# A triangle-and-gate pair kernel: the first seven tiles take their transposed input from the host, like all later ones, with other factors, order and queues

## The chip, the core and the metric

The kernel runs on one core of a Trainium2 chip. A core has a matrix engine (TensorE, PE in the profile; its weight loads are the row PEld), three engines for elementwise work (VectorE = DVE, ScalarE = ACT, GpSimd = POOL) and a queue engine (SyncE = SP) that only starts transfers. Each engine works through its own instruction list strictly in order; they wait for each other through semaphores. Transfers between the chip's memory and the on-chip buffers are started from the lists of SP, ACT or POOL. The metric is the device time of one execution in microseconds (us); less is better.

## The reference, cut to what matters

The input `x` is a 384 x 384 array of vectors with 128 channels, all float32. Two layers follow each other. The change touches only the first part of layer 0, written here with its names:

```python
z_n = _layernorm(z, norm_g, norm_b)                 # over the 128 channels
a = _linear(z_n, Wa, ba) * sigmoid(_linear(z_n, Wga, bga))
b = _linear(z_n, Wb, bb) * sigmoid(_linear(z_n, Wgb, bgb))
x = einsum('bijd,bjkd->bikd', a, b)                 # 128 products of 384 x 384 matrices
x = _layernorm(x, normo_g, normo_b)
out = z + _linear(x, Wo, bo) * sigmoid(_linear(z_n, Wgo, bgo))
```

Layer 1 then makes two projections of `out`, left (with the sum of two weight matrices, `W_left + W_eq`) and gate, multiplies them with the row sum of a third, projects the product, adds `out` and normalises.

## The kernel before, in words

The kernel has three stages. Stage 1 computes `a`, `b` and the gate of the output for all pixels and writes them to memory as A, B and G, together with Z = x + an output bias. Stage 2 (from L631) makes the 128 matrix products of A and B. Stage 3 (from L756) does the rest row by row. Only stage 1 is changed, and within it mostly its first tiles.

Stage 1 runs over 72 tiles of 128 rows x 16 columns x 128 channels (1 MB), each in four steps of four columns (512 vectors), so 288 calls of `step(s)` (L284); `n` is the tile and `t` the step in it. The program order of each engine is the order in which the Python code issues (the schedule is manual), so every position in `step` is a position in the engines' lists.

A projection needs the normalised input with the channels on the partitions. This comes about in two ways. In tiles 0 to 2 (`n < OLD`, L104), VectorE takes mean and variance (`statistics`, L154, with `bn_aggr`), POOL makes factor and offset (`norm_factors`, L161), ScalarE normalises column by column (`normalise`, L219), TensorE transposes four columns (`turn`, L238) and ScalarE copies the result out of PSUM (`turned_out`, L247). From tile 3 on, the transposed input `xT` is read from memory, where the host has put it (`fetch_turned`, L149). POOL computes one factor for each pixel from the raw statistics (`turned_factors`, L174, seven small instructions); ScalarE spreads the factors over the partitions with 16 copies of 32 x 16 values (`repeat`, L186); VectorE turns these into a full tile of factors with a 32 x 32 transpose and multiplies (`normalise_turned`, L196). Of the four columns of a step, POOL multiplies two (L216) and VectorE two. That the mean is subtracted is then the weights' work: they are multiplied with a centring matrix (`of_the_turned`, L381, called after steps 4, 5 and 6).

A step (L284 to L370) issues, in this order: on SP the next fetches where a tile begins; the statistics of columns some 36 ahead (VectorE) and the factors (POOL); the projections `ga` and `a` (TensorE, L308); the sigmoid of `ga` (ScalarE, L316); the sigmoid of the output gate of the step before (L257) and, after a tile, the store of G (started by POOL, L260); `at` (VectorE, L333) and, after a tile, the store of A (POOL, L337); `gb` and its sigmoid; in steps with `t == 1` the 16 copies; in the first tiles transpose and normalisation; `b` and `bt` (VectorE, L349); the output gate's projection (`gate_project`, L262: eight small products, L271, and `gs`, L273); the normalisation of step s+2; and the residual (`residual`, L229), which is one POOL addition over the whole tile (L235) followed by the start of the store of Z (L236). PSUM has six banks for the projections (`ppp`) and two for the transposes (`ppt`).

The buffer of an `x` tile is free once its statistics and its residual are done; there are three, so `fetch(n + 3)` waits for the residual of tile n. In the first 12 steps the residuals, factors and fetches have places of their own (`FIRST_RESIDUALS`, `FIRST_FACTORS`, `FIRST_FETCHES`, L278 to L283); later a tile's factors are issued at `t == 0` and its residual at `t == 1`.

Before step 0 (L411 to L467) the first quarter of tile 0 is loaded and normalised, the weights are scaled by `norm_g`, biases are corrected, and TensorE is kept busy with idle transposes (`keep_busy`, L443). `last_weights` (L393) prepares weights of layers 0 and 1 after steps 24, 25 and 26; among them are two additions of `W_left + W_eq` and of their biases on VectorE:

```python
nc.vector.tensor_tensor(w_left, w_left, w_eq, ALU.add)   # L399
nc.vector.tensor_tensor(b_left, b_left, b_eq, ALU.add)   # L400
```

Of the kernel before, what the change touches and what calls it, by code (L numbers as in the profile page):

```python
# [20 lines left out]
def kernel(ctx: ExitStack, tc: tile.TileContext, ins, out: bass.AP):  # L21
# [82 lines left out]
    OLD, SQ = 3, 32  # L104
# [6 lines left out]
    with tc.tile_pool(name="wprep", bufs=6) as wp, tc.tile_pool(name="p1s", bufs=3) as ps, tc.tile_pool(  # L111
        name="p1g", bufs=2
    ) as pgt, tc.tile_pool(name="p1z", bufs=4) as pz, tc.tile_pool(name="p1a", bufs=2) as pa_, tc.tile_pool(
        name="p1x", bufs=3
    ) as px, tc.tile_pool(name="p1b", bufs=1, side="right") as pb_, tc.tile_pool(name="p1t", bufs=2, space=PSUM) as ppt, tc.tile_pool(
        name="p1p", bufs=6, space=PSUM
    ) as ppp:
        tiles, turned, bts, gated, b_out_of = {}, {}, {}, {}, []

# [8 lines left out]
        def fetch_parts(n, parts):  # L128
# [10 lines left out]
            if n < OLD:  # L139
                tiles[n]["mv"] = ps.tile([P, CX, 2], FP, tag="mv", name=f"mv_{n}")  # L140
            else:
                tiles[n]["again"] = ps.tile([P, CX, P // SQ], FP, tag="again", name=f"again_{n}", bufs=2)
# [6 lines left out]
        def fetch_turned(n):  # L149
            if OLD <= n < NT:  # L150
                tiles[n]["zT"] = pz.tile([P, CX, P], FP, tag="zT", name=f"xT_{n}")
                nc.sync.dma_start(out=tiles[n]["zT"], in_=xT[n])

        def statistics(first, last):  # L154
            for k in range(first, min(last, NT * CX)):
                n, c = divmod(k, CX)
                nc.vector.bn_stats(tiles[n]["st"][:, c, :], tiles[n]["x"][:, c, :])
                if n < OLD:
                    nc.vector.bn_aggr(tiles[n]["mv"][:, c, :], tiles[n]["st"][:, c, :])

        def norm_factors(n, c0=0, c1=CX, beside=nc.gpsimd):  # L161
            if n >= NT:
                return
            if n >= OLD:
                return turned_factors(n, c0, c1)
            mv, rstd, off = (tiles[n][k][:, c0:c1] for k in ("mv", "rstd", "off"))
            beside.tensor_scalar(rstd, mv[:, :, 1], EPS, None, ALU.add)
            beside.tensor_scalar(off, mv[:, :, 0], -1.0, None, ALU.mult)
            nc.gpsimd.tensor_tensor(rstd, rstd, mhalf[:, 0 : c1 - c0], ALU.pow)
            nc.gpsimd.tensor_tensor(off, off, rstd, ALU.mult)  # L170
            if c0 == 0:
                tiles[n]["zT"] = pz.tile([P, CX, C], FP, tag="zT", name=f"zn_{n}")

        def turned_factors(n, c0, c1):  # L174

            st, v, d = (tiles[n][k][:, c0:c1] for k in ("st", "rstd", "off"))
            g = nc.gpsimd
# [6 lines left out]
            g.tensor_tensor(v, v, mhalf[:, 0 : c1 - c0], ALU.pow)  # L184

        def repeat(n):  # L186

            if n >= NT:
                return
            for b in range(P // SQ):  # L190
                for to in range(P // SQ):
                    nc.scalar.copy(
                        tiles[n]["again"][to * SQ : (to + 1) * SQ, :, b], tiles[n]["rstd"][b * SQ : (b + 1) * SQ, :]
                    )

        def normalise_turned(s):  # L196
# [6 lines left out]
            H = CT // 2 if s < S2 else 0  # L203
            for engine, k0, k1 in ((nc.gpsimd, 0, H), (nc.vector, H, CT)):
                if k0 == k1:
                    continue
                if k0 < H:
                    every = ps.tile([P, H, P], FP, tag="every", name=f"every_{s}")
# [10 lines left out]
        def normalise(n, t, cs=range(CT)):  # L219
            if n >= OLD:  # L220
                return
            g = tiles[n]
            for c in (t * CT + k for k in cs):
                nc.scalar.activation(
                    g["zT"][:, c, :], g["x"][:, c, :], AF.Identity,
                    bias=g["off"][:, c : c + 1], scale=g["rstd"][:, c : c + 1],
                )

# [8 lines left out]

        def turn(s, between=None):  # L238
            n, t = divmod(s, TS)
            ptr = ppt.tile([P, CT, P], FP, tag="ptr", name=f"ptr_{s}")  # L240
            for c in range(CT):
                nc.tensor.transpose(ptr[:, c, :], tiles[n]["zT"][:, t * CT + c, :], ident)
                if between:
                    between()
            turned[s] = ptr

        def turned_out(s):  # L247
            n, t = divmod(s, TS)
            zT = tiles[n]["zT"][:, t * CT : (t + 1) * CT, :]
            nc.scalar.copy(zT, turned[s])  # L250
            turned[s] = zT
# [11 lines left out]
        def gate_project(s):  # L263
# [8 lines left out]
            gs = ps.tile([P, CT, C], FP, tag="gs", name=f"gs_{s}")  # L272
# [4 lines left out]
        CATCH_UP = 3 * TS  # L277
        FIRST_FACTORS = {  # L278
            0: ((1, 0, 4),), 1: ((1, 4, 8),), 2: ((1, 8, 12),), 3: ((1, 12, 16),),
            4: ((2, 0, 4),), 5: ((2, 4, 12),), 6: ((2, 12, 16),), 7: ((3, 0, 8),), 9: ((3, 8, 16),),  # L280
        }
        FIRST_RESIDUALS, FIRST_FETCHES = {2: 0, 5: 1, 9: 2, 10: 3}, {2: 3, 5: 4, 9: 5}

        def columns_ahead(s):  # L284
            return CX + CT * s + 2 * min(max(s - TS, 0), 2 * TS)

        def step(s):
            n, t = divmod(s, TS)
            r0, c0 = place(n)
            if t == 0:  # L290
                if n >= OLD:
                    fetch(n + 3)
                fetch_turned(n + 2)
                if s >= CATCH_UP:
                    norm_factors(n + 1)
# [8 lines left out]
            ahead = (n + 1, t - 1) if t else (n, TS - 1)  # L304
# [14 lines left out]
            def statistics_ahead():  # L319
                statistics(columns_ahead(s), columns_ahead(s + 1))  # L320
                for factors in FIRST_FACTORS.get(s, ()):
                    norm_factors(*factors)

            if s:
# [6 lines left out]
            if 0 < s <= S2:  # L331
                gate(s - 1)
            nc.vector.scalar_tensor_tensor(  # L333
                at[:, t * CT : (t + 1) * CT, :], pa, bcol["a"], sga, ALU.add, ALU.mult
            )
            if t == TS - 1:
                nc.gpsimd.dma_start(out=A[:, c0 : c0 + CX, r0 : r0 + P], in_=at)  # L337
            pgb = proj("gb")
            sgb = sigmoid("b", pgb, by_row=True)
            if t == 1 and n + 1 >= OLD:  # L340
                repeat(n + 1)
            if s + 1 < OLD * TS:
                turn(s + 1)
                turned_out(s + 1)
            if s == 0:
                normalise(0, 2)
            normalise(*ahead)
# [6 lines left out]
            if s == 0:  # L354

                statistics_ahead()
            if s + 2 >= OLD * TS:
                normalise_turned(s + 2)
            if s < CATCH_UP:
                if s in FIRST_RESIDUALS:  # L360
                    residual(FIRST_RESIDUALS[s])
                if s in FIRST_FETCHES:
                    fetch(FIRST_FETCHES[s])
            elif t == 1:
# [12 lines left out]
        def scale_weight(k):  # L377
            raw[k], wT[k] = wT[k], ctile([P, P], "wT_" + k)
            nc.scalar.activation(wT[k], raw[k], AF.Copy, scale=ng)

        def of_the_turned():  # L381

            nc.vector.tensor_scalar(center, ident, -1.0 / C, None, ALU.add)
            yield
            for some in (("ga", "a"), ("gb", "b", "go")):
                centred = ppp.tile([P, CT, P], FP, tag="pk", name="centred_" + some[0])
                for n, k in enumerate(some):
                    nc.tensor.matmul(centred[:, n, :], lhsT=center, rhs=wT[k], start=True, stop=True)
                for n, k in enumerate(some):
                    nc.scalar.copy(wT[k], centred[:, n, :])  # L390
                yield

        def last_weights():  # L393
# [5 lines left out]
            nc.vector.tensor_tensor(w_left, w_left, w_eq, ALU.add)  # L399
            nc.vector.tensor_tensor(b_left, b_left, b_eq, ALU.add)  # L400
# [653 lines left out]
```

## Time and profile before

| | |
|---|---|
| median of three runs | 3198.97 us (3198.86 to 3198.99) |
| the profiled execution | 3198.7 us, of which 3196.9 us span |
| mean granted TensorE clock | 0.998 |
| busy shares of the span | PE 99%, DVE 85%, POOL 75%, ACT 63% |
| stage 1 | until about 1278 us, when the first product of stage 2 starts |
| one step of stage 1 in the steady part | 4.33 us |

Times of instructions are microseconds from the start of the span, followed by the duration. "x2" says that the profile shows two records for one instruction of the program. In brackets stands the time that the engine was idle just before, and which engine or transfer ended that idle time. Instructions overlap by a few hundredths to tenths of a microsecond, so the distance from one start to the next is what an instruction takes of its engine's time. PE is busy nearly throughout the span; the few places where it is not lie in the first 160 us, around 1235 and 1250 us, and at the very end.

### The profile page before, as it was taken

Reading aid. Unit: us, or ns where it says so; the run is one execution under the profiler, and the core shown is the slowest. Engines: PE = TensorE matmul, PEld = TensorE weight load, DVE = VectorE, ACT = ScalarE, POOL = GpSimd, SP = SyncE. Lnnn points to the kernel's source line nnn. Section 1 sums busy time; section 2 is a strip of 40 time slices with the busy share of each in tenths; the row PEclk is TensorE's granted clock in tenths of the full one; section 3 lists DMA queues with packets and bytes.
Section 4 is the critical chain, followed back from the end, with each engine's and each line's share of the span. In section 5 each row is a group of like instructions: output and inputs, shape, how many; then the busy total and the mean of one; then the engine's idle time right before and its main releaser. Section 6 shows DMA issues by size and latency. Waiting matters only on the chain.

```text
span 3196.9 us, 51440 instructions
## 1 busy us (share of the span) xinstructions
PE 3166.8 (99%) x14543; PEld 2087.0 (65%) x14543; DVE 2705.2 (85%) x8297; ACT 2008.9 (63%) x5225; POOL 2402.4 (75%) x2097
## 2 busy tenths in 40 slices
PE   9999999999999999999999999999999999999998
PEld 5555555555555555555555555788888888888886
DVE  6999999999999998455555555999999999999999
ACT  7566666666666665222222222588888888888888
POOL 6788888888888885455555555599999998888888
PEclk9999999999999999999999999999999999999999
DMA  6989999999999999999999999777777777777774
GB/s 217 368 341 363 370 369 367 361 362 353 372 370 364 369 363 335 350 314 311 313 311 313 310 309 290 248 267 264 259 268 262 259 270 257 260 270 258 263 269 156
DMA packets 426554, 982.75 MB, mean 307 GB/s; under 512 B 39696, under 2 KB 334224, under 8 KB 381088
## 3 DMA queue, kind: packets, MB, share of 16 engines
q1 hardware_dynamic: 385344, 752.64, 67.9%
q0 software_dynamic: 40352, 226.57, 18.0%
q8 instruction: 118, 1.93, 0.2%
q14 instruction: 164, 1.34, 0.1%
q10 hardware_dynamic: 576, 0.26, 0.0%
HBM read 526.39 MB, written 452.98 MB: 306 GB/s over the span
## 4 chain that ended last, share of the span: by engine, by line
PE 96%; POOL 1%; ACT 1%; DVE 1%; issue 1%; DMA 0%; ACTq 0%; POOLq 0%; DVEq 0%
PE pm L689 23%; PE py L529 8%; PE pf L797 8%; PE pleft L823 8%; PE pg L825 8%; PE pgo L271 8%; PE pga L308 7%; PE pgb L308 7%; PE pa L308 7%; PE pb L308 7%; PE ptr L552 4%; PE pg L836 0%; POOL rstd L184 0%; POOL acc L235 0%; ACT res L815 0%
## 5 line engine op out<-in xcount | busy, mean ns | idle before, releaser
L689 PE MATMUL pm<-ab 128*128 128x384 f32 x2304 | 743.9, 486 | 0.0
L709 POOL TENSOR_TENSOR acc<-acc,xd 128x384 f32<-128x384 f32 x381 | 379.8, 997 | 362.3 <-DVE xd L702 362.0
L689 PEld LDWEIGHTS pm<-ab 128*128 128x128 f32 x2304 | 437.5, 190 | 303.8
L707 ACT ACTIVATE sq<-xd 128x384 f32<-128x384 f32 x381 | 188.4, 495 | 541.3 <-DVE xd L702 541.3
L702 DVE TENSOR_TENSOR xd<-pm,acc 128x384 f32<-128x384 f32 x381 | 212.1, 557 | 342.8 <-POOL acc L709 321.7
L815 ACT ACTIVATE res<-res,off,rs 128x128 f32<-128x128 f32 x1134 | 475.0, 486 | 0.9
L316 ACT ACTIVATE sga<-pga,c_L_conv_bga 128x512 f32<-128x512 f32 x288 | 197.8, 687 | 345.6 <-PE pga L308 343.9
L535 DVE SCALAR_TENSOR_TENSOR py<-py,acc,gr 128x128 f32<-128x128 f32 x1152 | 384.1, 333 | 0.9
L271 PEld LDWEIGHTS pgo<-wT_go,xT 128*128 128x128 f32 x2208 | 287.6, 192 | 124.8 <-issue 78.4
L848 POOL TENSOR_TENSOR res<-res,r_L_conv_ln_bias 128x1536 f32<-128x1536 f32 (+1 forms) x96 | 326.6, 3402 | 7.5
L847 POOL TENSOR_TENSOR res<-res,r_L_conv_ln_scale 128x1536 f32<-128x1536 f32 (+1 forms) x96 | 326.8, 3405 | 0.5 <-ACT res L815 0.5
L235 POOL TENSOR_TENSOR acc<-xt,r_L_conv_b_out 128x2048 f32<-128x2048 f32 x72 | 326.7, 4538 | 0.0
L529 PE MATMUL py<-w_o,xr 128*128 128x128 f32 x2304 | 320.0, 275 | 0.0
L830 ACT ACTIVATE sg<-pg,c_L_conv_b_gate 128x384 f32<-128x384 f32 x384 | 223.0, 581 | 152.1 <-PE pg L825 103.0
L797 PE MATMUL pf<-w_o,h 128*128 128x128 f32 x2280 | 316.8, 275 | 0.0
L823 PE MATMUL pleft<-pairT,m_L_conv_W_left 128*128 128x384 f32 x768 | 311.6, 487 | 0.4 <-ACT pairT L553 0.4
L825 PE MATMUL pg<-pairT,m_L_conv_W_gate 128*128 128x384 f32 x768 | 310.6, 486 | 0.0
L540 DVE BATCH_NORM_STATS2 st<-res 128x6 f32<-128x128 f32 x1128 | 306.7, 272 | 0.0
L216 POOL TENSOR_TENSOR xT<-every,xT 128x256 f32<-128x256 f32 x260 | 190.2, 732 | 141.5 <-DVE every L212 136.0
L529 PEld LDWEIGHTS py<-w_o,xr 128*128 128x128 f32 x2304 | 288.4, 192 | 0.8
L271 PE MATMUL pgo<-wT_go,xT 128*128 128x128 f32 x2208 | 288.7, 275 | 0.0
L308 PE MATMUL pga<-xT,wT_ga 128*128 128x512 f32 x552 | 283.8, 596 | 4.9 <-POOL xT L216 3.2
(189 smaller groups left out, 6578.0 us busy)
## 6 DMA issues: line engine op xcount, KB each, us to landing
Z<-acc POOLq DMA_DIRECT2D x72, 1024.0 KB, 10.7
A<-at POOLq DMA_DIRECT2D x72, 1024.0 KB, 13.5
gr<-G SPq DMA_DIRECT2D x96, 768.0 KB, 5.8
zr<-Z SPq DMA_DIRECT2D x96, 768.0 KB, 7.2
xr<-X SPq DMA_DIRECT2D x96, 768.0 KB, 8.2
X<-xd SPq DMA_DIRECT2D x381, 192.0 KB, 5.8
xt<-in_x_dram SPq DMA_DIRECT2D x71, 1024.0 KB, 7.6
out_dram<-res SPq DMA_DIRECT2D x93, 768.0 KB, 4.1
```

What stands on the lines that cost most here:

```text
L235: nc.gpsimd.tensor_tensor(zb, tiles[n]["x"], over(b_out, CX), ALU.add)
L271: nc.tensor.matmul(pgo[:, c, :], lhsT=zT[:, c, :], rhs=wT["go"], start=True, stop=True)
L308: nc.tensor.matmul(pk, lhsT=wT[k], rhs=zT, start=True, stop=True)
L529: nc.tensor.matmul(py[:, q, :], lhsT=g["x"][:, i, q * P : (q + 1) * P], rhs=w_o0, start=True, stop=True)
L535: nc.vector.scalar_tensor_tensor(py[:, q, :], py[:, q, :], rs0[:, q, u : u + 1], g["g"][:, i, q, :], ALU.mult, ALU.mult)
L689: nc.tensor.matmul(products[d, ib].rearrange("p (s c) -> p s c", c=CG), lhsT=ab[:, 0, q, ib * P : (ib + 1) * P], rhs=b_of(d)[:, :, q, :], ...
L709: nc.gpsimd.tensor_tensor(s1[:, ib, :], s1[:, ib, :], xd, ALU.add)
L797: nc.tensor.matmul(pf[:, q, :], lhsT=h[:, q * P : (q + 1) * P], rhs=w_o, start=True, stop=True)
L815: nc.scalar.activation(g["res"][:, i, q, :], g["res"][:, i, q, :], AF.Identity, bias=g["off"][:, i, q : q + 1], scale=g["rs"][:, i, q : q ...
L823: nc.tensor.matmul(pleft, lhsT=w_left, rhs=pairT, start=True, stop=True)
L825: nc.tensor.matmul(pg[:, 0:N], lhsT=w_gate, rhs=pairT, start=True, stop=True)
L847: nc.gpsimd.tensor_tensor(flat, flat, over(ln_s, n * NB), ALU.mult)
```

## The change

All 72 tiles use the transposed input from the host. The old path of the first three tiles (`bn_aggr`, `normalise`, `turn`, `turned_out`, `OLD`) is gone. For this:

- In the first seven tiles (`FEW = 7`) the factors are spread otherwise. POOL gets one instruction more per call of `norm_factors`, which puts each factor into the column of its block of 32 rows (`apart`). TensorE multiplies this with a constant matrix of ones and zeros (`alike`), and ScalarE copies the small product out. These calls come in quarters, halves or whole tiles, at places listed in `FIRST_FACTORS` and `FIRST_REPEATS` by step, as (tile, first column, end) (15 small products inside steps, one before step 0).
- In steps 0 to 15 (`s < CLOSE`) the statistics are issued at the end of a step, VectorE alone multiplies all four columns, and the normalisation is issued one step ahead instead of two. In step 14 both the normalisation of step 15 and that of step 16 are issued; from then on it is two steps ahead, halved with POOL.
- The places of the first seven residuals are steps 6, 9, 11, 14, 15, 18 and 22 (before: 2, 5, 9, 10, then 13, 17, 21).
- There are four `x` buffers (before three); fetches are issued at the beginning of each tile. The transposed tiles 0, 1 and 2 are loaded too.
- The weights are centred before step 0, not after steps 5 and 6; `keep_busy` has fewer and other calls. The factors of the first quarter are computed on VectorE except for the power.
- From step 24 on, the 16 copies are in two runs of eight, after the sigmoid of `b` in steps with `t == 1` and before `at` in steps with `t == 2`.
- The two additions for the left weights are on GpSimd.

```diff
-            else:
-                tiles[n]["again"] = ps.tile([P, CX, P // SQ], FP, tag="again", name=f"again_{n}", bufs=2)
+            tiles[n]["again"] = ps.tile([P, CX, P // SQ], FP, tag="again", name=f"again_{n}")
+            if n < FEW:
+                tiles[n]["apart"] = ps.tile([P, CX, P // SQ], FP, tag="apart", name=f"apart_{n}", bufs=2)
...
+        def norm_factors(n, c0=0, c1=CX, g=nc.gpsimd):
...
             g.tensor_scalar(v, v, 1.0 / C, EPS, ALU.mult, ALU.add)
-            g.tensor_tensor(v, v, mhalf[:, 0 : c1 - c0], ALU.pow)
-
-        def repeat(n):
+            nc.gpsimd.tensor_tensor(v, v, mhalf[:, 0 : c1 - c0], ALU.pow)
+            if n < FEW:
+                each = [P, c1 - c0, P // SQ]
+                nc.gpsimd.tensor_tensor(
+                    tiles[n]["apart"][:, c0:c1], v[:, :, None].to_broadcast(each),
+                    of_block[:, None, :].to_broadcast(each), ALU.mult,
+                )
+
+        def repeat(n, c0=0, c1=CX, blocks=range(P // SQ)):
...
+            if n < FEW:
+                product = ppt.tile([P, CT, P], FP, tag="ptr", name=f"pagain_{n}_{c0}")[:, 0, 0 : (c1 - c0) * P // SQ]
+                flat = [t[:, c0:c1].rearrange("p c b -> p (c b)") for t in (tiles[n]["apart"], again)]
+                nc.tensor.matmul(product, lhsT=alike, rhs=flat[0], start=True, stop=True)
+                nc.scalar.copy(flat[1], product)
+                return
+            for b in blocks:
...
-            H = CT // 2 if s < S2 else 0
+            H = CT // 2 if CLOSE <= s < S2 else 0
...
-        CATCH_UP = 3 * TS
+        CATCH_UP = 6 * TS
         FIRST_FACTORS = {
...
+            0: (0, 12, 16), 1: (1, 0, 4), 2: (1, 4, 8), 3: (1, 8, 12), 4: (1, 12, 16), 5: (2, 0, 8), 7: (2, 8, 16),
+            8: (3, 0, 8), 10: (3, 8, 16), 12: (4, 0, 8), 13: (4, 8, 16), 16: (5, 0, 16), 20: (6, 0, 16),
         }
...
+        FIRST_REPEATS = {
+            0: (0, 4, 8), 1: (0, 8, 12), 2: (0, 12, 16), 3: (1, 0, 4), 4: (1, 4, 8), 5: (1, 8, 12), 6: (1, 12, 16),
+            7: (2, 0, 8), 9: (2, 8, 16), 10: (3, 0, 8), 12: (3, 8, 16), 14: (4, 0, 8), 15: (4, 8, 16),
+            18: (5, 0, 16), 22: (6, 0, 16),
+        }
+        FIRST_RESIDUALS = {6: 0, 9: 1, 11: 2, 14: 3, 15: 4, 18: 5, 22: 6}
+
+        def columns_done(s):
+
+            return 3 * CT if s < 0 else min(CX + 5 * s, CX + 20 + CT * s)
 
         def step(s):
...
             if t == 0:
-                if n >= OLD:
-                    fetch(n + 3)
                 fetch_turned(n + 2)
+                fetch(n + 3)
...
-            if s:
+            if s >= CLOSE:
                 statistics_ahead()
             pga, pa = proj("ga"), proj("a")
...
             if 0 < s <= S2:
                 gate(s - 1)
+            if t == 2 and s >= CATCH_UP:
+                repeat(n + 1, blocks=(2, 3))
             nc.vector.scalar_tensor_tensor(
                 at[:, t * CT : (t + 1) * CT, :], pa, bcol["a"], sga, ALU.add, ALU.mult
             )
             if t == TS - 1:
                 nc.gpsimd.dma_start(out=A[:, c0 : c0 + CX, r0 : r0 + P], in_=at)
+            if s in FIRST_REPEATS:
+                repeat(*FIRST_REPEATS[s])
+            if s + 1 < CLOSE:
+                normalise_turned(s + 1)
             pgb = proj("gb")
             sgb = sigmoid("b", pgb, by_row=True)
-            if t == 1 and n + 1 >= OLD:
-                repeat(n + 1)
-            if s + 1 < OLD * TS:
-                turn(s + 1)
-                turned_out(s + 1)
-            if s == 0:
-                normalise(0, 2)
-            normalise(*ahead)
+            if t == 1 and s >= CATCH_UP:
+                repeat(n + 1, blocks=(0, 1))
             pb = proj("b")
...
-            if s == 0:
-
+            if s < CLOSE:
                 statistics_ahead()
-            if s + 2 >= OLD * TS:
+            if s + 2 >= CLOSE:
                 normalise_turned(s + 2)
...
+            if s in FIRST_RESIDUALS:
+                residual(FIRST_RESIDUALS[s])
+            elif s >= CATCH_UP and t == 1:
                 residual(n + 1)
...
-            nc.vector.tensor_tensor(w_left, w_left, w_eq, ALU.add)
-            nc.vector.tensor_tensor(b_left, b_left, b_eq, ALU.add)
+            nc.gpsimd.tensor_tensor(w_left, w_left, w_eq, ALU.add)
+            nc.gpsimd.tensor_tensor(b_left, b_left, b_eq, ALU.add)
...
-        keep_busy(30)
+        keep_busy(20)
         statistics(0, CT)
         norm_factors(0, 0, CT, nc.vector)
...
+        scale_weight("ga")
+        scale_weight("a")
+        centre(("ga", "a"))
+        keep_busy(9)
+        for k in ("gb", "b", "go"):
             scale_weight(k)
...
+        repeat(0, 0, CT)
+        centre(("gb", "b", "go"))
+        statistics(CT, 2 * CT)
+        norm_factors(0, CT, 2 * CT)
+        normalise_turned(0)
...
+        statistics(2 * CT, 3 * CT)
+        norm_factors(0, 2 * CT, 3 * CT)
```

## The prediction

> **What bounds the kernel now.** I read the busy shares and the chain of work that ended last first, then the stretches of the first 160 us beside a steady one, then the instructions in order of time there.
>
> ```profile
> PE 3166.8 (99%) x14543; PEld 2087.0 (65%) x14543; DVE 2705.2 (85%) x8297; ACT 2008.9 (63%) x5225; POOL 2402.4 (75%) x2097
> PE 96%; POOL 1%; ACT 1%; DVE 1%; issue 1%; DMA 0%; ACTq 0%; POOLq 0%; DVEq 0%
> ```
>
> TensorE is the bound, so the change can only move TensorE's work or its waits. These are few. In the stretches (PE, PEld, DVE, ACT, POOL busy, clock, DMA) they show beside 300 to 600 us, where TensorE has no gap:
>
> ```profile
> 60.00:70.00 10.00, 6.05 (x18) 3.17 (x18) 2.85 (x10) 6.12 (x20) 4.78 (x2) 0.83 0.48 132
> 80.00:90.00 10.00, 8.72 (x32) 4.70 (x31) 6.89 (x19) 7.14 (x22) 9.63 (x10) 1.00 1.00 386
> 150.00:160.00 10.00, 8.57 (x32) 4.63 (x31) 9.93 (x25) 5.65 (x17) 7.73 (x12) 1.00 0.86 337
> 300.00:600.00 300.00, 300.00 (x1109) 167.30 (x1108) 272.58 (x694) 187.75 (x484) 243.68 (x258) 1.00 0.94 361
> ```
>
> The instructions in order of time give each gap its cause:
>
> ```profile
> 10.17 1.10 PE L308 MATMUL pga<-zn,wT_ga 128*128 128x512 f32 x2
> ...
> 63.99 2.08 PE L308 MATMUL pga<-zn,wT_ga 128*128 128x512 f32 x2 [3.95 <-ACT zn L250]
> ...
> 85.68 1.12 PE L308 MATMUL pga<-xT,wT_ga 128*128 128x512 f32 x2 [1.28 <-POOL xT L216]
> ...
> 145.84 1.13 PE L308 MATMUL pgb<-xT,wT_gb 128*128 128x512 f32 x2 [1.48 <-DVE at L333]
> ...
> 159.06 1.13 PE L308 MATMUL pga<-xT,wT_ga 128*128 128x512 f32 x2 [1.28 <-POOL xT L216]
> ```
>
> These are the projections `ga` of steps 0, 10, 14 and 30, and `gb` of step 27. After 159.06 TensorE has no gap until 1235. So the change is a matter of when step 30 begins; a steady step takes 4.33 us.
>
> **What the change takes away.** In steps 0 to 10 four transposes go. They begin at 17.82 and the next product at 18.25: 0.43 each, 4.8 in all (a step with them took 4.77 us). The centring in steps 5 and 6 goes (five products of 0.22, and 0.36 of wait: 1.5). The 16 copies before step 10, which held up ScalarE and cost 3.95 of idle time, go too, and with them a slow stretch: from 63.99 the products `ga` and `a` took 3.34 instead of 1.72 us. The additions of L399 and L400 leave VectorE:
>
> ```profile
> 139.86 4.49 DVE L400 TENSOR_TENSOR c_L_conv_b_left<-c_L_conv_b_left,c_L_conv_b_eq 128x1 f32<-128x1 f32 x1
> 148.17 0.14 DVE L406 TENSOR_SCALAR c_L_conv_b_out<-c_L_conv_b_out 128x1 f32<-128x1 f32 x1
> ```
>
> A 128x1 instruction took 4.49 us, from just after the beginning to just after the end of POOL's residual (139.71, 4.62 us long); another of that size took 0.14. VectorE stayed late until step 30: `ga` of step 27 began at 142.48, three steps are 13.0, and step 30 came at 159.06, so it cost 3.6. On POOL both additions take some 0.5, behind the residual of tile 7, where POOL has idle time (1.87 us before 139.03).
>
> **What it adds, until step 14.** Each small product is taken at 0.22, the distance between the products of the biases at 9.50 and 9.72; 128 columns also take 0.22 (39.07 to 39.29), so it can't be much more. Start: the first factors take six VectorE instructions of some 0.2 after the statistics, as late as L168 before (5.9), then the power 1.04 and the new placing (`apart`): 7.3. Product, copy, transpose (0.75) and product of four columns (0.69) bring step 0 to 9.9; before it was 10.17. A quarter of xT (256 KB) is now loaded ahead of `norm_g` and the weights; at the 200 GB/s of that stretch that is up to 1.3, so 9.4 to 11.2. VectorE has in a step of this part, start to start: `at` 0.65, transpose 0.75, product 0.61, `bt` 0.66, `gs` 0.61, five statistics 0.98: 4.26, under the 4.55 of a step with a small product. So step 14 could begin at 9.9 + 14 x 4.33 + 12 x 0.22 (eleven small products and one for the gate's bias) + 0.4 (a wait in step 9) = 73.6. Before it began at 85.68: a gain of 12.1.
>
> **What it adds on POOL, and where the gain goes.** POOL's instructions by their starts:
>
> ```profile
> 101.65 0.74 POOL L216 TENSOR_TENSOR xT<-every,xT 128x256 f32<-128x256 f32 x1
> 104.41 0.72 POOL L216 TENSOR_TENSOR xT<-every,xT 128x256 f32<-128x256 f32 x1 [2.02 <-DVE every L212]
> 105.09 4.55 POOL L235 TENSOR_TENSOR acc<-xt,r_L_conv_b_out 128x2048 f32<-128x2048 f32 x1
> 109.94 0.59 POOL L236 DMA_DIRECT2D Z<-acc  x1 [0.30 <-POOL acc L235]
> 110.55 0.74 POOL L216 TENSOR_TENSOR xT<-every,xT 128x256 f32<-128x256 f32 x1
> 111.82 1.23 POOL L337 DMA_DIRECT2D A<-at  x1 [0.52 <-DVE at L333]
> ```
>
> A residual with its store takes 5.46 (105.09 to 110.55), a store of A 1.25, of G 0.67, a half tile's product 0.70. Factors of 16 columns took 4.55 (79.70 to 84.25), of 8 columns 3.2 (47.61 to 50.81). The placing has no row. The nearest are 128x16 at 0.2 and 128x256 at 0.7; for 32 to 64 values I take 0.35 to 0.4, near the smaller one: 3.55 for eight columns, 4.95 for 16.
>
> From step 5 on POOL has no pause. The factors of tile 2 wait for column 39, some 6.2 after step 5 begins at 32.9: 39.1. Then, in program order: factors 3.55, residual 0 5.46, A 1.25, factors 3.55 (52.9; step 9 wants them at 52.6), G 0.67, factors 3.55, residual 1 5.46, factors 3.55, A 1.25, residual 2 5.46, G 0.67, factors of tile 4 3.55: done at 77.0. The small product of step 14, queued on TensorE before `gb`, could run at 75.3: a wait of 1.8. The next factors end at 80.6, before step 15 wants them.
>
> Now the halves come back to POOL, and two residuals, the store of A and the factors of tile 5 are issued among them. The half of step 16 ends at 82.9 (VectorE reaches it after `gs` and statistics of step 14). Behind it: residual 3 5.46, A 1.25, half of step 17 0.70 (90.3), residual 4 5.46, factors of tile 5 4.95, G 0.67, half of step 18 0.74: 102.1. TensorE would begin step 17 at 88.8 and waits 1.6; step 18 at 94.7 and waits 7.5, until 102.2. Before, step 18 began at 85.68 + 17.3 = 103.0. **Of the gain of 12.1, 0.8 is left.** This cover gone, every microsecond that POOL is later is one for TensorE.
>
> After a wait of 7.5 the clock: the row at 63.99 priced one of 3.95 at 1.6 more, and I take that. Residuals 5 and 6 come at `t == 2`, followed by A, a half and 16 columns of factors. That is the order that delayed steps 13 and 14 before: 0.8 (74.70 + 4.33 to 79.81) and 1.5 (84.14 to 85.68). It comes twice, once with the placing (0.4): with 0.87 and 1.96, 0.87 and 1.52 from the same sums, 5.2. From step 18 to 30: 12 x 4.33 + 2 small products 0.4 + 2 products of the last weights 0.4 + 1.6 + 5.2 = 59.6, so step 30 begins at 161.8, against 159.06: 2.7 later.
>
> [...]
>
> **Copies in two runs.** ScalarE's 16 copies take 3.63, eight 1.82. In steps with `t == 2`, counted from `ga`: sigmoid at 1.12, gate 1.71, copies 2.26, sigmoid of `b` at 4.08, so `bt` at 4.82, before at 4.50 (1202.48 less 1197.98). `at` no longer waits (1201.39 becomes 1200.80). TensorE needs neither: its banks ask for `bt` at 7.8. Nothing is gained in the steady part; around 1235 and 1250, where VectorE is the limit, about 0.2. Four x buffers instead of three change no wait that the trace shows, and the loads of the first tiles (3 MB more) fall into 20 to 30 us, where the DMA engines were 0.13 busy.
>
> **Sum.** 2.7 - 0.2 = 2.5 on the profiled execution's 3198.7, which is 0.3 below the median of the runs: 3201.5. About 0.2% (6.4 us) is what a measurement of this kernel can tell from no change.
>
> **Rivals.**
> - POOL is not the limit after all, and step 18 doesn't wait: the 7.5 and 1.6 fall away, 3192.4; if steps 14, 17, 21, 22, 25 and 26 don't wait either, 3184. For it: POOL was idle for a quarter of the span. Against it: the 19.9 us between the halves of steps 16 and 18 are all rows of this trace, start to start, and would have to be 12.4.
> - Slower: the split copies. `bt` at `t == 2` waits 0.25 more on VectorE per tile (1.35 after its predecessor is done, against 0.67 + 0.43 before `at` and `bt`). Elsewhere in a tile it has some 0.8 of pauses (1193.03 to 1198.18). From 0.5 more per tile TensorE begins to wait in each of 62 tiles, 6 us for each further 0.1: 3208 and up.
> - Slower: POOL and the start at their upper ends, placing 0.7 (seven of them in POOL's row: +2.3), start 11.2 (+1.3), clock twice (+1.6): 3206.7. A late x tile 5 (fetched after residual 1, at 62; the slowest landing of such a load was 11.9; wanted about 75) would add to the same wait.
>
> **How the numbers follow.** Forecast case 0.78, POOL not the limit 0.08, split copies 0.05, upper ends 0.09. Placing at 0.2 (-1.0), start at 9.4 (-0.5), waits as in the rows (-0.5), no clock loss (-1.6) give 3198; the other side 3206.7. With part of the first rival: 3197 to 3207. Faster by over 0.2% only in the first rival, slower in the last two.
>
> **What would show it.** Right: `ga` of step 14 near 74 to 76, a TensorE wait of 6 to 9 us near 95 to 103 ended by POOL's L216 product, POOL without pause from 39 to 102, the clock low after it, shorter waits of the same kind near 117, 123, 137 and 143, no 4.5 us addition. Wrong: no such wait (gain stays), or TensorE gaps in every tile after 200 us.

## The result and the profile after

The changed kernel takes 3209.74 us (median of six runs, 3209.54 to 3211.61) against 3198.93 (3198.80 to 3199.23) for the kernel before in the same measurement: ratio 1.0034, 95% interval 1.0024 to 1.0044. It is 10.8 us slower. The forecast was 3201.5 with a range of 3197 to 3207, most likely no change, so forecast and range were both wrong. The profiled execution took 3209.6 us, its span 3207.8.

Busy shares and the engines' shares of the chain that ended last, in the kernel after:

```profile
PE 3170.3 (99%) x14521; PEld 2086.6 (65%) x14521; DVE 2693.8 (84%) x8275; ACT 1987.8 (62%) x5115; POOL 2409.3 (75%) x2145
...
PE 91%; POOL 4%; ACT 2%; DVE 2%; issue 1%; DMA 0%; SPq 0%; ACTq 0%; POOLq 0%; DVEq 0%
```

TensorE was busy 3166.8 us before and is now 3170.3, and the span grew by 10.9: the time is idle time of TensorE and a slower clock. In the chain, POOL has 4% instead of 1%. The same stretches as in the prediction, and 95 to 105 us (PE, PEld, DVE, ACT, POOL busy, clock, DMA share, GB/s):

```profile
60.00:70.00 10.00, 10.00 (x44) 6.12 (x43) 9.47 (x22) 3.87 (x8) 9.23 (x12) 1.00 0.96 342
80.00:90.00 10.00, 9.16 (x37) 5.14 (x35) 9.53 (x29) 3.86 (x7) 7.78 (x7) 1.00 0.72 263
95.00:105.00 10.00, 2.67 (x5) 1.17 (x4) 2.92 (x10) 0.32 (x1) 7.18 (x13) 0.64 1.02 419
150.00:160.00 10.00, 10.00 (x41) 5.70 (x40) 9.34 (x27) 4.42 (x7) 6.23 (x14) 1.00 0.50 183
300.00:600.00 300.00, 299.80 (x1109) 167.20 (x1108) 267.92 (x693) 190.56 (x485) 242.84 (x259) 1.00 0.90 355
```

Two things are to be seen. From 95 to 105 TensorE works 2.67 of 10 us, and its clock is down to 0.64. And the steady stretch is not quite full: 299.80 instead of 300.00, with less transferred (355 against 361 GB/s). How much each costs is read from the starts of `ga`, step by step, in the two traces:

| from the start of `ga` to the next (us) | before | after | difference |
|---|---|---|---|
| span start to step 0 | 10.17 | 9.80 | -0.4 |
| step 0 to 14 | 75.51 | 64.33 | -11.2 |
| step 14 to 30 | 73.38 | 89.81 | +16.4 |
| step 30 to 44 | 60.67 | 60.68 | 0.0 |
| step 44 to 271 | 982.58 | 988.37 | +5.8 |
| step 271 to 287 | 58.19 | 58.39 | +0.2 |
| sum | | | +10.9 |

So the first 14 steps win what was foretold, the next 16 lose more than that, and then the 227 steps to 271, which were to cost nothing, lose 5.8.

**The start.** TensorE's rows of steps 0, 14, 18, 19 and 30:

```profile
9.80 1.10 PE L297 MATMUL pga<-xT,w_four 128*128 128x512 f32 x2
...
74.13 1.02 PE L297 MATMUL pga<-xT,w_four 128*128 128x512 f32 x2
...
102.50 2.08 PE L297 MATMUL pga<-xT,w_four 128*128 128x512 f32 x2 [7.33 <-POOL xT L226]
104.37 1.91 PE L297 MATMUL pa<-xT,w_four 128*128 128x512 f32 x2
...
109.91 1.02 PE L297 MATMUL pga<-xT,w_four 128*128 128x512 f32 x2
...
163.94 1.13 PE L297 MATMUL pga<-xT,w_four 128*128 128x512 f32 x2 [0.36 <-POOL xT L226]
```

Step 18 waits 7.33 us for POOL, and its products then take 2.08 and 1.91 us instead of 1.02: step 19 comes 7.41 after step 18, 3.08 more than a steady step. POOL's rows before it:

```profile
82.41 0.73 POOL L226 TENSOR_TENSOR xT<-every,xT 128x256 f32<-128x256 f32 x1 [1.83 <-DVE every L222]
83.09 4.54 POOL L235 TENSOR_TENSOR acc<-xt,r_L_conv_b_out 128x2048 f32<-128x2048 f32 x1
...
89.79 0.74 POOL L226 TENSOR_TENSOR xT<-every,xT 128x256 f32<-128x256 f32 x1
90.47 4.54 POOL L235 TENSOR_TENSOR acc<-xt,r_L_conv_b_out 128x2048 f32<-128x2048 f32 x1
...
97.57 2.93 POOL L181 TENSOR_TENSOR rstd<-rstd,mhalf 128x16 f32<-128x16 f32 x1
...
101.72 1.41 POOL L226 TENSOR_TENSOR xT<-every,xT 128x256 f32<-128x256 f32 x2
```

The halves of steps 16, 17 and 18 (82.41, 89.79, 101.72) stand behind the residuals of tiles 3 and 4 and the factors of tile 5, as in the prediction's list.

**The steady part.** SP's list does nothing but start transfers, and it has waits of its own. First those of the kernel before, then those of the kernel after, from 160 to 1200 us (in total, times, longest):

```profile
SPq L144 <- POOL acc L235: 613.3, 45, 15.9
SPq L370 <- DVE bt L349: 283.8, 15, 22.6
```

```profile
SPq L355 <- DVE bt L338: 510.6, 15, 36.3
SPq L160 <- PE pgo L256: 204.8, 30, 7.2
SPq L160 <- DVE xT L226: 159.5, 30, 9.2
```

Before, the load of `x` waited in three tiles of four for the residual that frees its buffer (45 times, up to 15.9 us). With four buffers that wait is gone. SP runs on to the next thing that can stop it, the first store of a group's B, and stands there up to 36.3 us; the loads behind it in the list stand with it. Then all go at once. SP's rows in one such place of the kernel after:

```profile
207.97 1.27 SPq L147 DMA_DIRECT2D xt<-in_x_dram  x1
245.01 0.33 SPq L355 DMA_DIRECT2D B<-bt  x1
245.44 1.13 SPq L160 DMA_DIRECT2D xT<-in_xT_dram  x1
246.67 1.63 SPq L147 DMA_DIRECT2D xt<-in_x_dram  x1
248.35 1.26 SPq L355 DMA_DIRECT2D B<-bt  x1
249.71 1.14 SPq L160 DMA_DIRECT2D xT<-in_xT_dram  x1
250.94 1.41 SPq L147 DMA_DIRECT2D xt<-in_x_dram  x1
252.40 0.57 SPq L355 DMA_DIRECT2D B<-bt  x1
```

Nothing for 37 us, then seven transfers of 1 MB in 7.4. The DMA engines swing with it; just before the burst they stand nearly still, and TensorE has gaps (columns as above):

```profile
225.00:230.00 5.00, 5.00 (x19) 2.69 (x18) 3.77 (x11) 2.00 (x3) 3.85 (x9) 1.00 1.01 410
230.00:235.00 5.00, 4.83 (x18) 2.59 (x17) 4.35 (x12) 2.00 (x5) 3.62 (x3) 1.00 0.69 269
235.00:240.00 5.00, 5.00 (x19) 2.75 (x18) 3.81 (x10) 4.79 (x18) 3.31 (x2) 1.00 0.29 113
240.00:245.00 5.00, 3.99 (x16) 2.14 (x15) 4.57 (x12) 2.29 (x5) 3.62 (x4) 1.00 0.35 146
```

The transfers, median us from issue to landing (300 to 1100 us), before and after:

```profile
xt<-in_x_dram SPq DMA_DIRECT2D x46, 1024.0 KB, 7.8
xT<-in_xT_dram SPq DMA_DIRECT2D x46, 1024.0 KB, 11.6
G<-gt POOLq DMA_DIRECT2D x46, 1024.0 KB, 11.0
```

```profile
xT<-in_xT_dram SPq DMA_DIRECT2D x47, 1024.0 KB, 19.0
xt<-in_x_dram SPq DMA_DIRECT2D x47, 1024.0 KB, 23.3
G<-gt POOLq DMA_DIRECT2D x46, 1024.0 KB, 12.3
```

In the kernel after, no engine waits for a landed load from 200 to 1200 us even so. It is stores under way while the DMA engines work off a burst that come late: A and G have two buffers each, and two kinds of waits for landed stores appear in that time that the kernel before doesn't have at all:

```profile
ACT gt L242 <- DMA G<-gt: 4.6, 4, 1.5
...
DVE at L324 <- DMA A<-at: 1.2, 1, 1.2
```

They sum to 5.8, like the loss from step 44 to 271, but that is chance: in e2 below such waits sum to 11.4 and the loss is 4.8. ScalarE and VectorE have some slack, and what counts is which waits reach TensorE. The way there can be followed once:

```profile
207.78 1.23 POOL L328 DMA_DIRECT2D A<-at  x1 [0.94 <-DVE at L324]
...
229.71 0.75 DVE L324 SCALAR_TENSOR_TENSOR at<-pa,c_L_conv_ba,sga 128x512 f32<-128x512 f32 x1 [1.19 <-DMA A<-at]
...
243.63 1.13 PE L297 MATMUL pga<-xT,w_four 128*128 128x512 f32 x2 [1.01 <-POOL xT L226]
```

The store of A at 207.78 went out beside two loads (207.55 and 207.97) and landed 21.8 us later; half of the stores of A from 160 to 1200 us landed within 15.8. The burst above comes after it; it is under way while the DMA engines work off the one before, seven transfers from 173.55 to 180.31: the DMA share is 1.00 to 1.03 in every 5 us from 175 to 230. `at` of step 44 (229.71) needs that buffer and starts 1.19 late, VectorE's next instructions come later, POOL stands idle for 3.04 until 236.69, its residual starts at 237.38, and the half that step 48 needs stands behind it (242.84). TensorE waits 1.01 there (243.63). That this is the way in every place is argued from this one.

### The profile page after: what moved, and what is told of

Read it like the earlier page. It is cut to its first block, busy times and chain, and to the rows that moved or that the text cites. A ratio compares the mean times of both kernels' runs of the same rounds, so it can differ in the third digit from the quotient of the medians.

```text
span 3207.8 us, 51449 instructions
## 1 busy us (share of the span) xinstructions
PE 3170.3 (99%) x14521; PEld 2086.6 (65%) x14521; DVE 2693.8 (84%) x8275; ACT 1987.8 (62%) x5115; POOL 2409.3 (75%) x2145
## 4 chain that ended last, share of the span: by engine, by line
PE 91%; POOL 4%; ACT 2%; DVE 2%; issue 1%; DMA 0%; SPq 0%; ACTq 0%; POOLq 0%; DVEq 0%
PE pm L689 23%; PE py L529 8%; PE pf L797 8%; PE pleft L823 8%; PE pg L825 8%; PE pgo L256 7%; PE pga L297 7%; PE pa L297 6%; PE pgb L297 6%; PE pb L297 6%; PE ptr L552 4%; POOL rstd L181 1%; POOL acc L235 1%; ACT again L202 1%; POOL xT L226 0%
## 5 line engine op out<-in xcount | busy, mean ns | idle before, releaser
L535 DVE SCALAR_TENSOR_TENSOR py<-py,acc,gr 128x128 f32<-128x128 f32 x1152 | 449.9, 391 | 0.9 <-PE py L529 0.2
L256 PEld LDWEIGHTS pgo<-w_go,xT 128*128 128x128 f32 x2304 | 300.1, 192 | 130.6 <-issue 99.9
L540 DVE BATCH_NORM_STATS2 st<-res 128x6 f32<-128x128 f32 x1128 | 372.4, 330 | 0.0
L338 DVE SCALAR_TENSOR_TENSOR bt<-pb,c_L_conv_bb,sgb 128x512 f32<-128x512 f32 x288 | 215.0, 747 | 122.4 <-ACT sgb L305 101.8
L297 PE MATMUL pga<-xT,w_four 128*128 128x512 f32 x576 | 299.0, 601 | 17.3 <-POOL xT L226 15.1
L256 PE MATMUL pgo<-w_go,xT 128*128 128x128 f32 x2304 | 301.2, 275 | 0.0
L297 PE MATMUL pgb<-xT,w_four 128*128 128x512 f32 x576 | 296.2, 596 | 0.0
```

The costliest lines, as they stand in the source:

```text
L256: nc.tensor.matmul(pgo[:, c, :], lhsT=zT[:, c, :], rhs=wT["go"], start=True, stop=True)
L297: nc.tensor.matmul(pk, lhsT=wT[k], rhs=zT, start=True, stop=True)
L535: nc.vector.scalar_tensor_tensor(py[:, q, :], py[:, q, :], rs0[:, q, u : u + 1], g["g"][:, i, q, :], ALU.mult, ALU.mult)
L540: nc.vector.bn_stats(b["st"][:, k, q, :], b["res"][:, k, q, :])
```

## Experiments

Three theories were to be told apart. **P**: in the first tiles the order of POOL's list costs what the new path wins. **D**: with four `x` buffers the loads lose the wait that spaced them, and come in bursts. **C**: the copies in two runs make VectorE late. Rounds are shared with runs of the kernel before on the same chip, 3198.8 to 3199.1 in the median. "Late" is how much longer than 4.329 the step before took, from one `ga` to the next.

**e1: the left weights on GpSimd, alone.** In the kernel before:

```diff
-            nc.vector.tensor_tensor(w_left, w_left, w_eq, ALU.add)
-            nc.vector.tensor_tensor(b_left, b_left, b_eq, ALU.add)
+            nc.gpsimd.tensor_tensor(w_left, w_left, w_eq, ALU.add)
+            nc.gpsimd.tensor_tensor(b_left, b_left, b_eq, ALU.add)
```

> The kernel before, with only the two additions for the left weights moved to GpSimd. If a 128x1 addition on VectorE really held that engine for the 4.5 us of a residual, and VectorE then stayed late until step 30, the time falls by 3.6 us, to 3195.3, and the TensorE gaps at 145.8 and 159.1 go. Rival: the lateness was hidden but for its first wait, then 1.5 to 1.7 us, 3197.3. If GpSimd pays for it instead: no change, 3198.9.

Measured: 3196.95 (3196.36 to 3197.88), ratio 0.9993 (0.9983 to 1.0002): 1.85 less, not clear of the interval, and nearest to the rival's 3197.3. In the trace steps 28 and 29 are no longer late (before 1.74 and 0.31), but step 27 is as late as before (0.44, before 0.45), and step 30 still waits 1.02 for POOL, before 1.28. POOL had been late there on its own account. Steps 14 to 30 take 70.96 instead of 73.38. So the move is worth 1.9 in the median and 2.4 in the trace of the 3.6 that the prediction gave it: 3.6 was the lateness of step 30, of which VectorE's addition was only one cause.

**e2: the copies in one run again.** In the changed kernel:

```diff
-            if t == 2 and s >= CATCH_UP:
-                repeat(n + 1, blocks=(2, 3))
...
-                repeat(n + 1, blocks=(0, 1))
+                repeat(n + 1)
```

> The changed kernel with the 16 copies in one run again, after the sigmoid of b at t == 1. Between steps 30 and 271 the changed kernel loses 5.7 us in small waits that the kernel before doesn't have. Theory C (the split copies make VectorE wait 1.55 us for the sigmoid of b in each tile and use up its pauses): most of the 5.7 go, 3204 to 3205. Theory D (with four x buffers SP is no longer held back by the residuals, runs ahead to a store of B, waits there up to 36 us, and then issues two tiles' loads in one burst, behind which the stores of A and G land late): the loss stays, 3209 to 3210. If both are needed, either cure gives 3204.

Measured: 3206.7 (3205.74 to 3211.22), ratio 1.0025 (1.0016 to 1.0035). That lies between the two expectations and fits neither. Steps 44 to 271 take 987.37, 4.8 more than before the change and only 1.0 less than after it: most of that loss is not the copies'. The rest of what e2 wins lies elsewhere: step 30 is no longer 0.52 late, step 19 is 2.31 late instead of 3.08 after the same wait, and steps 271 to 287 take 0.2 less.

**e3: the loads kept behind the residual.** In the changed kernel, with its four buffers, from tile 5 on `x` is asked for one tile further ahead, so that its buffer is again the one that a residual has just to free, and it stands ahead of `xT`:

```diff
-                fetch_turned(n + 2)
-                fetch(n + 3)
+                if n < 5:
+                    fetch_turned(n + 2)
+                fetch(n + 3 if n <= 5 else n + 4)
+                if n == 5:
+                    fetch(9)
+                if n >= 5:
+                    fetch_turned(n + 2)
```

> The changed kernel with four x buffers, but from tile 5 on the fetch is one tile further ahead and stands before that of xT, so that SP waits for the residual of tile n again, as it did with three buffers. Theory D: the bursts go (x lands in 8 us instead of 22, A never later than 17), and with them the 5.7 us between steps 30 and 271: 3204. Theory C: the loss stays, 3209 to 3210. The first 24 steps should not change: step 18 begins at 102 to 103 in both.

Measured: 3203.97 (3203.38 to 3204.65), ratio 1.0015 (1.0006 to 1.0024). SP's longest waits in e3 are again those of the kernel before:

```profile
SPq L147 <- POOL acc L235: 602.0, 45, 15.8
SPq L360 <- DVE bt L343: 287.7, 15, 21.1
```

`x` lands in 6.9 us, no engine waits for a landed store any more, and steps 44 to 271 take 983.58. Of the 5.8 only 1.0 is left. The loads go out after a longer wait and the kernel is faster: theory D.

**e4: the residual of tile 4 two steps later.** In the changed kernel:

```diff
-        FIRST_RESIDUALS = {6: 0, 9: 1, 11: 2, 14: 3, 15: 4, 18: 5, 22: 6}
+        FIRST_RESIDUALS = {6: 0, 9: 1, 11: 2, 14: 3, 17: 4, 18: 5, 22: 6}
```

> The changed kernel with residual 4 issued in step 17 instead of step 15, all else the same. Theory P (GpSimd works through a row that ends with the half tile of step 18; every microsecond of it is one for TensorE): step 18 begins 5.5 us earlier, near 97.0, the wait before it is 1.9 instead of 7.3, and the slow clock after it (3.1 us) doesn't come, so up to 8.5 us by step 20; residuals 4 and 5 then stand close together and give back 0 to 5 in steps 19 to 22: 3201 to 3206. Rival (the wait at step 18 has another cause, a late load or VectorE): step 18 stays near 102.5 and the time near 3209.7.

Measured: 3203.81 (3198.81 to 3208.50), ratio 1.0016 (1.0007 to 1.0026); the profiled execution is the fastest of them. Step 18 there:

```profile
96.64 1.12 PE L297 MATMUL pga<-xT,w_four 128*128 128x512 f32 x2 [1.86 <-POOL xT L226]
97.61 1.02 PE L297 MATMUL pa<-xT,w_four 128*128 128x512 f32 x2
```

The wait falls from 7.33 to 1.86, the clock stays up (granted 1.00 from 95 to 105 us, 0.64 in the changed kernel), and step 30 begins at 155.36 instead of 163.94. One entry of a list was worth 8.6 us in this execution, and 5.9 in the median.

**e5: factors and copies earlier, POOL's products later.** The remaining waits of steps 15 to 30 are of the same kind, so the first tiles were rearranged, in the changed kernel:

```diff
-    SQ, FEW, CLOSE = 32, 7, 4 * TS
+    SQ, FEW, CLOSE = 32, 7, 6 * TS
...
-            8: (3, 0, 8), 10: (3, 8, 16), 12: (4, 0, 8), 13: (4, 8, 16), 16: (5, 0, 16), 20: (6, 0, 16),
+            8: (3, 0, 8), 10: (3, 8, 16), 12: (4, 0, 8), 13: (4, 8, 16), 15: (5, 0, 8), 16: (5, 8, 16), 18: (6, 0, 8), 20: (6, 8, 16),
...
-            18: (5, 0, 16), 22: (6, 0, 16),
+            17: (5, 0, 8), 18: (5, 8, 16), 20: (6, 0, 8), 22: (6, 8, 16),
...
-        FIRST_RESIDUALS = {6: 0, 9: 1, 11: 2, 14: 3, 15: 4, 18: 5, 22: 6}
+        FIRST_RESIDUALS = {6: 0, 9: 1, 11: 2, 14: 3, 17: 4, 19: 5, 21: 6}
```

> The changed kernel with VectorE alone multiplying until step 23 (instead of 15), the factors of tiles 5 and 6 in two halves at steps 15, 16, 18 and 20, their copies a step earlier, and the residuals of tiles 4, 5 and 6 at steps 17, 19 and 21. Theory P (GpSimd's list: products of steps 17 to 26 stand behind factors and residuals): the waits at steps 15 to 30, 20.1 us over the pitch of 4.329 in the changed kernel, fall below 5, against VectorE's steps of 4.6 instead of 4.33 from 14 to 20 (6 x 0.27 = 1.6); step 30 at 163.94 - 13 = 149 to 153, and the total, with the loads still in bursts, 3209.7 - 12 = 3195 to 3200. Rival (VectorE is what the steps wait for, whoever multiplies): step 30 stays above 155 and the total above 3201. Theory D alone: the loss between steps 44 and 271 stays at 3 to 6.

Measured: 3200.98 (3197.64 to 3206.89), ratio 1.0006 (0.9997 to 1.0015). Steps 14 to 30 take 77.39 instead of 89.81. That is still 8.1 above 16 steady steps (16 x 4.329 = 69.3), not below 5 as expected: steps 15 (1.67), 23 (2.05), 28 (1.13) and 30 (1.41) are late, and steps 16, 18, 19 and 21, which follow a small product, by 0.22 to 0.42. Step 30 begins at 151.50, within the 149 to 153 expected; the median is 1 us above the expected 3195 to 3200. Steps 44 to 271 take 989.46, 6.9 more than before the change: the bursts are still there.

**e6: e3 and e4 together.**

> The changed kernel with the residual of tile 4 at step 17 and, from tile 5 on, the load of x put ahead of the load of x turned and kept behind GpSimd's residual. Theory: the two losses are apart and add: 3209.7 - 5.7 (loads, as measured alone) - 8.6 (start at step 30, as its profiled run showed alone) = 3195.4, range 3194 to 3198; steps 44 to 271 in 983.6, step 30 at 155.4. Rival (the second loss returns elsewhere when the first goes): 3198 to 3204.

Measured: 3198.46 (3197.03 to 3199.22), ratio 0.9997 (0.9988 to 1.0006), at the rival's end of the expectation. The steady part is mended as before (984.24), but step 30 comes at 157.66, not at 155.36 as in the profiled execution of e4. Of these 2.3 us, 0.6 are there at step 14 and 1.7 are the clock after step 18 (granted 0.83 from 95 to 105 us, 1.00 in e4), in e6:

```profile
97.24 1.56 PE L302 MATMUL pga<-xT,w_four 128*128 128x512 f32 x2 [1.88 <-POOL xT L226]
98.60 1.91 PE L302 MATMUL pa<-xT,w_four 128*128 128x512 f32 x2
```

Step 19 is 2.01 late here and 0.32 late in e4, after the same wait (1.88 and 1.86). The expectation had added the best execution of e4, not its median.

**e7: four `x` buffers in the kernel before.** To make room, the spread factors and the gated tile have two buffers instead of three.

```diff
-        name="p1x", bufs=3
+        name="p1x", bufs=4
...
-                    every = ps.tile([P, H, P], FP, tag="every", name=f"every_{s}")
+                    every = ps.tile([P, H, P], FP, tag="every", name=f"every_{s}", bufs=2)
...
-            gs = ps.tile([P, CT, C], FP, tag="gs", name=f"gs_{s}")
+            gs = ps.tile([P, CT, C], FP, tag="gs", name=f"gs_{s}", bufs=2)
```

> The kernel before with four x buffers instead of three (and two instead of three of the gated tile and the spread factors, to make room), all else as it was. Theory D: the queue's wait for the residual goes, it runs ahead to the next group's store and loads land in bursts: x lands in 15 to 25 us instead of 7, and steps 44 to 271 take 984 to 988 instead of 982.6: 3200 to 3204. Rival (the burst needs the change's other order, x turned ahead of x, or its divided copies): 3199 within 0.5, steps 44 to 271 in 982.6 to 983.

Measured: 3204.50 (3201.72 to 3206.88), ratio 1.0016 (1.0006 to 1.0025). SP's waits in e7:

```profile
SPq L370 <- DVE bt L349: 530.3, 15, 38.3
SPq L144 <- POOL acc L235: 309.8, 30, 14.1
```

The kernel before becomes 5.4 us slower by one buffer more: SP stands up to 38.3 us before the store of B, `x` lands in 20.0 us, and steps 44 to 271 take 989.23 in the profiled execution, which at 3206.88 is the slowest of the ten. Neither the divided copies nor the other order of `x` and `xT` is needed for it. (The smaller numbers of `every` and `gs` buffers are in it too; e9 below has them, and its steps 44 to 271 take 982.59, as before the change, so they are not the cause.) The way to TensorE is in part another one than above: besides ScalarE and VectorE, which wait for landed stores of G and A (12.9 and 3.0), POOL's products wait 16.7 us in nine places for a landing that the trace names as a store of B; which transfer it really was is not shown.

**e8: e5 and e3 together.**

> The early factors and the loads kept behind the residual together. Theory P and D: 3195 to 3200 less 5: 3189 to 3195, the lowest of all. Rival (the early part is bound by VectorE, so that only the loads count): 3196 or more.

Measured: 3191.80 (3191.14 to 3192.11), ratio 0.9976 (0.9967 to 0.9986), as expected and faster than either kernel. Step 30 begins at 150.18, steps 44 to 271 take 983.97.

**e9: e8 with the copies in one run** (the edit of e2).

> Early factors and loads held back, and the 16 copies of the factors in one run at the second step of a tile, as in the kernel before. If the divided copies still cost something (steps 82, 134, 186 and 238 are 0.15 to 0.17 late, VectorE waits 83.6 us for sgb), 3191.8 - 0.6 to - 1.4 = 3190.4 to 3191.2, steps 44 to 271 in 982.6 to 983.4 instead of 983.97. If VectorE's wait is slack, 3191.8 within 0.4.

Measured: 3189.06 (3188.43 to 3191.83), ratio 0.9970 (0.9959 to 0.9982), the best of all and 1.3 below the expected range: 10.0 less than the kernel before and 20.7 less than the changed one. (e9 and e10 ran on another chip than the rest; the kernel before takes 3199.10 there and 3199.13 in e8's rounds.) Steps 44 to 271 take 982.59, as long as before the change, so that the divided copies cost 1.4 there, and step 30 begins 0.5 earlier. VectorE's largest wait from 300 to 1100 us, in e8 and then in e9, shows the cause (theory C, at a small price):

```profile
DVE bt L343 <- ACT sgb L310: 66.4, 46, 1.7
```

```profile
DVE at L327 <- ACT sga L310: 26.6, 46, 0.6
```

**e10: e8 with the two additions for the left weights on VectorE.**

> Early factors and loads held back, with the two additions of the left weights back on VectorE. If their 4.5 us under GpSimd's residual stop TensorE as in the kernel before (1.74 at step 28 and what follows), 3191.8 + 1.9 to + 3.6 = 3193.7 to 3195.4; if steps here have the slack, 3191.8 within 0.5.

Measured: 3193.57 (3193.30 to 3194.20), ratio 0.9982 (0.9973 to 0.9991), 1.8 above e8, at the lower end of the expectation and much as in e1; steps 14 to 30 take 78.26 instead of 75.90. The second addition in e10, and the residual beside it on POOL:

```profile
133.44 4.48 DVE L388 TENSOR_TENSOR c_L_conv_b_left<-c_L_conv_b_left,c_L_conv_b_eq 128x1 f32<-128x1 f32 x1
```

```profile
133.29 4.61 POOL L235 TENSOR_TENSOR acc<-xt,r_L_conv_b_out 128x2048 f32<-128x2048 f32 x1
```

Step 28 is 1.64 late and step 30 1.57; in e8 only step 30 is, by 1.11.

## Why the prediction was wrong, step by step

On the profiled execution the forecast was 3198.7 + 2.5 = 3201.2, and 3209.6 came: 8.4 too little. By the table that is 2.1 at step 30, 5.8 from there to step 271 and 0.4 after it.

- **"Four x buffers instead of three change no wait that the trace shows": this step failed, with 4.8 of the 8.4.** (That is e3's gain from step 44 to 271; in the medians e3 is 5.8 below the changed kernel.) The trace did show the wait, in SP's own waits: 45 of up to 15.9 us. I had looked at the engines' waits, where a full buffer of loads shows nothing as long as the data are in time. The wait was no cost but the spacing of the loads. e7 shows the loss from the buffer alone, e3 its end when the wait is restored.
- **"TensorE needs neither" (copies in two runs) failed with 1.0 to 1.4, and 0.5 more at step 30.** The prediction had `bt` 0.25 later per tile. After the change VectorE waits there for `sgb` 1.4 us each time (72.5 us in 51 waits from 300 to 1100 us, a stretch of some 46 tiles). The rival had VectorE's wait right and its price wrong: 1.0 us from step 44 to 271 (e2 against the changed kernel) or 1.4 (e9 against e8), not 6 us for each 0.1. TensorE did not begin to wait in every tile: in e3, without bursts, only steps 82, 134, 186 and 238 are over 0.12 late, by 0.13 to 0.15.
- **The clock was mis-sized by 1.3.** After the wait of 7.33, step 19 came 3.08 late. Some 0.2 of that is the small product, which the sum has apart; for the clock I had taken 1.6 from the one row there was, after a gap of 3.95. The same wait of 7.33 made step 19 2.31 late in e2 and 3.35 in e3, small product included, so no single figure would have held. The "clock twice" of the slower rival (3.2) was an estimate that no row of the kernel before shows; the 2.9 here is nearer to it than to 1.6.
- **Start and step 14: right.** Step 0 at 9.80 (foretold 9.9), step 14 at 74.13 (73.6). The gain over before was 11.55, not 12.1.
- **POOL's order, steps 14 to 18: right.** Step 17 waited 1.42 (1.6) and step 18 7.33 (7.5), ended by POOL's product, and step 18 began at 102.50 (102.2). The placing, which had no row, took 0.24 and 0.29 us (0.35 to 0.4 taken). e4 shows the cause: moving one residual takes the wait from 7.33 to 1.86. The rival in which POOL is not the limit fell.
- **Steps 21, 22, 25 and 26: right.** They were late by 0.78, 1.90, 0.78 and 1.58 (0.87, 1.96, 0.87 and 1.52 foretold), but steps 23, 27 and 30, which the sum left out but for their small products, were late by 0.32, 0.55 and 0.52. The 0.52 at step 30 is the divided copies': in e2 and e9 it is gone. With the clock, step 30 came at 163.94, not 161.8.
- **The left weights: right in the operation, wrong in the price of the old one.** On POOL they take 0.47 and 0.19 us and there is no 4.5 us addition, but moving them is worth 1.8 to 2.4 (e1, e10; medians and traces), not 3.6. The 3.6 was the whole lateness at step 30, and part of it is POOL's own; the forecast's sum, which has no wait after step 26, took it as gone.
- **"About 0.2" gained around 1235 and 1250: wrong.** Steps 271 to 287 took 0.2 more; e2 and e9, with the copies in one run, take 58.18 and 58.21, as before.

The rows gave the start to within 0.6 us up to step 18; the range failed at a term set to zero without a view of the queue that it changes.

## What to carry to other kernels

A wait of a queue that only starts transfers may be what spaces them, as SP's 45 waits of up to 15.9 us did here: before adding a buffer, read that queue's own waits and ask where it will stop next, and what stands behind that place. When work is taken from the start of a pipeline, the list of the engine that fed it must move too: much the same operations lost 16.4 us in one order (steps 14 to 30) and 1.5 in another, with VectorE taking over POOL's products for eight more steps (e9: 74.87 against 73.38 before). And a forecast of two edits together adds medians, not the best execution of one of them (e6).

## What the runs showed of the hardware that was not expected

- A 128x1 addition on VectorE took almost as long as the GpSimd instruction beside which it started, in the three traces that have it there: 4.48 us beside a residual of 4.61 in e10, 4.49 beside one of 4.62 in the kernel before and in e7, against 0.19 on POOL in the changed kernel. What held it no run shows. For the kernel moving the addition is worth only 1.8 to 2.4 us.
- In e6 the clock fell to half speed after an idle time of only 1.88 us, with one of 1.42 a step earlier: `pa` of step 18 took 1.71 us of TensorE's time (98.60 to 100.31), that of step 17 0.86, and the granted clock was 0.83 from 95 to 105 us. In e4 the clock stayed up after the same two (1.86 and 1.42): `pa` took 0.85 (97.61 to 98.46), and the granted clock was 1.00 from 95 to 105. Step 19 was 2.01 late in e6 and 0.32 in e4, where most of it is the small product. So equal waits cost unequally here; why, no run shows.
- With bursts a kernel's time often varied more: the kernel before spread over 1.5 us in the rounds of e7, and over 5.2 with one buffer more (e7); e5 spread over 9.3, and over 1.0 with the loads held back (e8). It is no rule: the changed kernel, with bursts, spread over 2.1 in its six runs, and e9, without, over 3.4.
